# The adjacency product of the last graph layer in two float32r parts, with the matrix loaded again in pieces by POOL's queue

## Chip, cores and metric

The kernel runs on one core of a Trainium2 chip. The time is device microseconds of one execution of the whole program, as the median of three runs; lower is better.

## What is computed

A network of four layers on 16 graphs (B) of 1024 nodes (N) with 128 features (D). Each layer normalises the rows of x, applies relu, computes a graph operation with the adjacency matrix, and adds the result to x:

```python
# layer 0: three sage convolutions on a thinned adjacency (adj with some neighbours skipped)
# layer 1: attention, 4 heads of 32 features
scores = einsum('chqd,chkd->chqk', q, k) * SCALE + log(max(adj, EPS))
out    = softmax(scores) @ v @ Wo.T + bo
# layer 2: graph attention, 4 heads; e = leaky_relu(s_i + s_j), masked by adj, softmax over i
out    = einsum('bijh,bihd->bjhd', alpha, Wh)
# layer 3: normalised product of the adjacency
A_hat  = adj + eye(n);  d_inv = sum(A_hat, 2) ** -0.5
h      = einsum('bnm,bmf->bnf', d_inv[:, :, None] * A_hat * d_inv[:, None, :], h)
out    = h @ W.T + b
```

The adjacency holds zeros and ones. All inputs and the result are float32, and products keep about float32's precision: where a matrix operand is exact in a narrow type (the adjacency), the other operand is split into several narrow parts whose products are added up in PSUM.

## The kernel before, in words

The program has three stages: the thinning of the adjacency (up to some 680 us), the convolutions (to some 1550 us), and the attention stage, `attentions_plain`, in which layers 1 to 3 run for all 16 graphs. (A slower path behind a test at the end isn't taken with these inputs.) Only the attention stage is changed.

The attention stage is a set of seven jobs, written as Python generators, which go over the graphs b one after another and run interleaved:

- `matrices`: loads a graph's adjacency in eight row blocks (tile `a`, SP's queue), turns it into a one-byte tile `A` of 128 x 8 x 1024 (L1318, ACT), checks that it is zero or one (L1322, DVE) and symmetric (L1329 to L1335, PE and ACT; `junk2` takes the unused output). Four tiles `A` (pool `f_adj`).
- `before`: ends layer 0 and makes q, k, v of layer 1 (L1362 to L1391).
- `attend`: scores and exponentials of layer 1 (L1416 to L1429). It reads `A`.
- `values`: the weighted sums and the denominators (L1452), the reciprocal of the denominators into `rden` (L1458), and their product into `oT` (L1460).
- `positive` and `gat`: layer 2. `positive` makes masks `pm` on DVE (L1503), `gat` multiplies them with bf16 parts on PE (L1563 and L1578), and sums the results on DVE (L1566, L1581). POOL multiplies `vals` with exponentials `ex` (L1543). Both jobs read `A`.
- `gcn`: layer 3. `normal` normalises the rows of x, scaled by d_inv, into `g` (bn_stats on DVE, a power on POOL at L1275, eight activations on ACT at L1282). POOL adds the bias to x (L1610). Then `g` is split into three bf16 parts, half by half (L1615 to L1621: ACT, DVE, ACT, DVE). For each half `hf` of the columns, 8 row blocks times 3 parts are multiplied with `A` (L1632, 24 matmuls of 512 columns), and 4 blocks times 3 parts with the identity, which adds the eye of A_hat (L1636, 12 matmuls of 128 columns). ACT copies the sum to `aggT` (L1639), a product with W follows (L1303), and DVE and POOL finish the rows.

The order of instructions on each engine is fixed when the program is built. Each job yields, ahead of every step, the engine, a planned duration, the time at which its inputs are planned to be there, and whether it takes or gives back one of two PSUM banks (`bank`, pool `f_sum`). `in_order` always takes the step that can start first by that plan; among equals PE's steps come later and the job furthest behind its share goes first:

```python
start = max([free[engine], needs] + [min(pools[pool]) for pool, change in tiles(j) if change > 0])
key = (start, engine == "PE", j["did"] / j["per"] + j["lag"])
```

On the chip every engine then runs its own list strictly in that order, and waits on semaphores where an operand isn't there or a buffer isn't free. DMAs on SP's queue are issued by an engine that computes nothing; DMAs issued by POOL stand in line with POOL's arithmetic. A job also waits for others while the plan is made; `matrices` and `before` start graph b as follows:

```python
while done["gcn"] < b - 3 or done["attend"] < b - 1:
    yield
```

Of the kernel before, what the change touches and what calls it, by code (L numbers as in the profile page):

```python
# [5 lines left out]

F32 = mybir.dt.float32
F16 = mybir.dt.float16
BF16 = mybir.dt.bfloat16
F8 = mybir.dt.float8e4  # L10
# [8 lines left out]
P = 128  # L19
# [1194 lines left out]
def attentions_plain(tc, x, spill, final, ready_weights, adj, deg, trouble, eye, out, scores, bound, reach):  # L1214
    nc = tc.nc
    with ExitStack() as ctx:
# [3 lines left out]
        psa = ctx.enter_context(tc.tile_pool(name="f_acc", bufs=2, space=PSUM))  # L1220
        psg = ctx.enter_context(tc.tile_pool(name="f_sum", bufs=2, space=PSUM))
        xp = ctx.enter_context(tc.tile_pool(name="f_x", bufs=4))
        adp = ctx.enter_context(tc.tile_pool(name="f_adj", bufs=4))
        lp = ctx.enter_context(tc.tile_pool(name="f_load", bufs=2))
        ep = ctx.enter_context(tc.tile_pool(name="f_exp", bufs=2))
        pmp = ctx.enter_context(tc.tile_pool(name="f_pos", bufs=2))
        w2 = ctx.enter_context(tc.tile_pool(name="f_work2", bufs=2))
        w1 = ctx.enter_context(tc.tile_pool(name="f_work1", bufs=1))

        ident = cp.tile([P, P], F32, name="ident")  # L1230
        nc.sync.dma_start(ident, eye)
        ident16 = cp.tile([P, P], BF16, name="ident16")
        nc.vector.tensor_copy(ident16, ident)
        minus16 = cp.tile([P, P], BF16, name="minus16")
# [8 lines left out]
        def bank(pool=psg, name="sum"):  # L1243
            return pool.tile([P, HN], F32, name=name)
# [63 lines left out]
        def matrices():  # L1308

            for b in range(B):  # L1310
                while done["gcn"] < b - 3 or done["attend"] < b - 1:
                    yield
                m = adp.tile([P, NB, N], F8, name="A")
                for i in range(NB):
                    t = yield "ACT", 1.3, 0.0, 0
                    a = lp.tile([P, N], F32, name="a")
                    nc.sync.dma_start(a, adj[b, i * P:(i + 1) * P, :])
                    nc.scalar.activation(m[:, i, :], a, AF.Relu, accum_out=deg[:, b, i:i + 1], saturate=False)  # L1318
                    yield "DVE", 1.32, 0.0, 0
                    junk = lp.tile([P, N], F8, name="junk", bufs=1)  # L1320

                    nc.vector.scalar_tensor_tensor(junk, a, 0.0, a, op0=ALU.is_gt, op1=ALU.not_equal,  # L1322
                                                   accum_out=trouble[:, b, i, 0:1], saturate=False)
                    for hf in range(2):
                        w = min(HN, (i - 4 * hf) * P)
                        if w > 0:
                            e = yield "PE", 0.1 + w / 1024, t, 1
                            ps = bank()
                            nc.tensor.matmul(ps[:, :w], ident16, m[:, i, hf * HN:hf * HN + w], start=True, stop=False)  # L1329
                            for j in range(w // P):  # L1330
                                nc.tensor.matmul(ps[:, j * P:(j + 1) * P], m[:, 4 * hf + j, i * P:(i + 1) * P], minus16,
                                                 start=False, stop=j == w // P - 1)
                            yield "ACT", 0.8, e, -1
                            junk = lp.tile([P, HN], BF16, name="junk2", bufs=1)
                            nc.scalar.activation(junk[:, :w], ps[:, :w], AF.Abs, accum_out=trouble[:, b, i, 1 + hf:2 + hf])  # L1335

                t = yield "DVE", 0.2, 0.0, 0
                nc.vector.tensor_scalar(dinv[:, b], deg[:, b], 1.0, None, op0=ALU.add)
                yield "POOL", 1.7, t, 0
                nc.gpsimd.tensor_tensor(dinv[:, b], dinv[:, b], minus_half, op=ALU.pow)  # L1340
                A[b] = m
# [92 lines left out]
        def values():  # L1434

            free, n = 0.0, 0
            for b in range(B):
                oT = w1.tile([P, N], F32, name="oT")
                for hf in range(2):
                    cols = slice(hf * HN, (hf + 1) * HN)  # L1440
                    for k in range(NB):
                        while n not in exps:
                            yield
                        es, e = exps[n]
                        e = yield "PE", 1.85, max(e, free), 0
                        if k == 0:
                            acc, den = [bank(psa, "acc") for _ in range(2)]
                        va = ready[b][4]
                        for ps, one in ((acc, False), (den, True)):
                            for hd in range(H):  # L1450
                                r = slice(hd * HD, (hd + 1) * HD)
                                nc.tensor.matmul(ps[r], ones if one else va[:, k, r], es[:, hd],  # L1452
                                                 start=k == 0, stop=k == NB - 1)
                        taken[n] = e
                        n += 1
                    rden = w1.tile([P, HN], F32, name="rden")
                    e = yield "DVE", 3.4, e, 0
                    nc.vector.reciprocal(rden, den)  # L1458
                    free = yield "DVE", 0.7, e, 0
                    nc.vector.tensor_tensor(oT[:, cols], acc, rden, op=ALU.mult)  # L1460
                xt = ready[b][1]
                t = yield from natural_times(oT, free, wo, "DVE", lambda c, ps: nc.vector.tensor_tensor(
                    xt[:, c, :], xt[:, c, :], ps, op=ALU.add))
# [43 lines left out]
        def gat():  # L1507
            for b in range(B):
# [26 lines left out]
                shared[b, "sc"] = (hT, minus, m)  # L1535

                e = yield "ACT", 0.5, e, 0
                ex = small.tile([P, 2, NB, 8], F32, name="ex", bufs=2)
                nc.scalar.activation(ex[:, 0], sc, AF.Exp)
                nc.scalar.activation(ex[:, 1], sc, AF.Exp, scale=SLOPE)  # L1540
                for k in range(2):
# [60 lines left out]
        def gcn():  # L1602
            for b in range(B):
# [4 lines left out]
                t = yield from normal(xt, t, g, dinv[:, b])  # L1608
                yield "POOL", 2.4, 0.0, 0
                nc.gpsimd.tensor_tensor(xt, xt, per_col(b3r), op=ALU.add)  # L1610
                parts = w1.tile([P, 3, NB, D], BF16, name="gparts")
                for m in range(2):
                    half = slice(4 * m, 4 * m + 4)
                    e = yield "ACT", 0.6, t, 0
                    nc.scalar.copy(parts[:, 0, half], g[:, half])  # L1615
                    e = yield "DVE", 0.7, e, 0
                    nc.vector.tensor_tensor(g[:, half], g[:, half], parts[:, 0, half], op=ALU.subtract)
                    e = yield "ACT", 0.6, e, 0
                    nc.scalar.copy(parts[:, 1, half], g[:, half])
                    e = yield "DVE", 0.7, e, 0  # L1620
                    nc.vector.tensor_tensor(parts[:, 2, half], g[:, half], parts[:, 1, half], op=ALU.subtract)  # L1621
                t = e
                aggT = w1.tile([P, N], F32, name="aggT")
                for hf in range(2):
                    cols = slice(hf * HN, (hf + 1) * HN)
                    for m in range(NB):
                        if m % 2 == 0:
                            e = yield "PE", 1.3, t, 0 if m else 1
                            if m == 0:
                                ps = bank()  # L1630
                        for k in range(3):
                            nc.tensor.matmul(ps, parts[:, k, m, :], A[b][:, m, cols], start=m == 0 and k == 0, stop=False)  # L1632
                    e = yield "PE", 0.7, t, 0
                    for m in range(4):
                        for k in range(3):
                            nc.tensor.matmul(ps[:, m * P:(m + 1) * P], parts[:, k, 4 * hf + m, :], ident16,  # L1636
                                             start=False, stop=m == 3 and k == 2)
# [190 lines left out]
```

## Time and profile before

| | |
|---|---|
| three runs | 3955.3, 3951.44, 3953.14 us |
| median | 3953.14 us |
| profiled execution, first to last instruction | 3957.5 us |
| mean granted clock of PE | 0.941 |
| PE busy, 1500 us to the end (2457 us) | 2128.5 us |
| DVE, ACT, POOL busy there | 1662.0, 1593.6, 389.7 us |
| L1632, 768 matmuls of 512 columns | 176.3 us busy |
| L1636, 384 matmuls of 128 columns | 26.7 us busy |
| L1615 and L1619, ACT casts, 32 each | 19.7 and 19.9 us |
| L1617 and L1621, DVE subtractions, 32 each | 36.4 and 23.2 us |

The profile is of one execution, whose own time the page gives only as the span from the first to the last instruction. It lists busy time by engine, groups of instructions by line of the kernel with what ended the idle time before them, and the chain of work that ended last. Mean durations of matmuls contain a drain that overlaps the next one, so paces are read from start to start. For DMAs from POOL's queue there is also the time from issue to landing; for SP's and ACT's queues there is none.

### The profile page before, as it was taken

The page shows a single profiled execution, that of the slowest core. Times are in us where ns is not written, and L with a number is a line of the kernel's source. Part 1 is how long each engine was busy: PE and PEld are TensorE (multiplying, and loading weights), DVE is VectorE, ACT ScalarE, POOL GpSimd, SP SyncE. Part 2 cuts the span into 40 slices and gives each one's busy share as a digit, 9 for nine tenths or more (in the row PEclk, how much of TensorE's full clock was granted, in tenths as well). Part 3 has the DMA queues.
Part 4 walks back from the last instruction along what each step waited for, and adds up shares of the span by engine and source line. Part 5 has one row for each costly group of instructions (what it writes and reads, how often), then busy time and mean ns, then how long its engine had stood idle before and what let it go on. Part 6 is the DMA issues. An engine that isn't in the chain of part 4 may idle for free.

```text
span 3957.5 us, 65696 instructions
## 1 busy us (share of the span) xinstructions
PE 3428.3 (87%) x26692; PEld 1955.4 (49%) x26692; DVE 2524.1 (64%) x4782; ACT 2391.7 (60%) x3961; POOL 804.0 (20%) x680
## 2 busy tenths in 40 slices
PE   4888887899999987788989998998898899898875
PEld 2556565445555556334445544544454454554443
DVE  4988784553343444337767766876775776686676
ACT  3788764453333345786677677667667667667630
POOL 6545521210000011101112021112102112211111
PEclk9999986999999998899999999999999999999987
DMA  9632223443333313311222221212212222121000
GB/s 108 42 22 16 13 82 119 155 169 129 129 120 133 130 61 126 100 59 38 75 62 62 70 75 54 68 62 67 68 60 65 64 65 65 54 65 49 17 22 23
DMA packets 182498, 293.19 MB, mean 74 GB/s; under 512 B 77468, under 2 KB 124456, under 8 KB 173992
## 3 DMA queue, kind: packets, MB, share of 16 engines
q1 hardware_dynamic: 91944, 221.69, 17.4%
q0 software_dynamic: 79728, 24.66, 7.7%
q10 hardware_dynamic: 10512, 42.54, 2.7%
q8 instruction: 211, 3.46, 0.4%
q14 instruction: 103, 0.84, 0.1%
HBM read 287.98 MB, written 51.19 MB: 86 GB/s over the span
## 4 chain that ended last, share of the span: by engine, by line
PE 60%; DVE 18%; ACT 11%; DMA 5%; POOL 4%; issue 3%; SPq 0%; ACTq 0%; POOLq 0%; DVEq 0%
PE g L1040 12%; PE acc L1452 11%; PE sum L1578 8%; PE t L1421 5%; PE sum L1632 4%; PE sum L1563 4%; DVE pm L1503 3%; DMA rows<-in_adj_dram 3%; ACT e L1429 2%; PE sum L1365 2%; DVE rows L882 2%; DVE r L835 2%; PE o L1089 2%; PE o L1090 2%; DVE rden L1458 1%
## 5 line engine op out<-in xcount | busy, mean ns | idle before, releaser
L1429 ACT ACTIVATE e<-t 128x1024 f32<-128x1024 f32 x512 | 506.8, 1022 | 516.6 <-PE t L1421 467.3
L1503 DVE SCALAR_TENSOR_TENSOR pm<-dst,minus,A 128x1024 fp8e4<-128x1024 f32 x512 | 668.2, 1329 | 9.0 <-DMA dst<-scores 9.0
L1040 PE MATMUL g<-C,parts 128*128 128x512 fp8e4 x2304 | 524.8, 383 | 18.7 <-DVE aggT L1042 11.6
L1416 ACT ACTIVATE t<-A 128x2048 f32<-128x2048 fp8e4 x256 | 483.0, 1887 | 4.0 <-ACT dst L1483 0.6
L1578 PEld LDWEIGHTS <-pm 128*128 128x128 fp8e4 x4096 | 349.3, 98 | 178.0 <-issue 141.4
L1578 PE MATMUL sum<-parts,pm 128*128 128x198 bf16 x4096 | 399.5, 252 | 42.1 <-DVE pm L1503 29.3
L1452 PE MATMUL acc<-e,va 128*32 128x512 f32 x2048 | 356.7, 633 | 64.2 <-ACT e L1429 61.5
L1040 PEld LDWEIGHTS <-parts 128*128 128x128 bf16 x2304 | 224.1, 99 | 265.6 <-issue 9.7
L1452 PE MATMUL acc<-e,ones_hd 128*32 128x512 f32 x2048 | 343.5, 615 | 0.7 <-DVE oT L1460 0.7
L1421 PE MATMUL t<-qT,kT 32*128 32x512 f32 x2048 | 299.0, 654 | 21.2 <-ACT t L1416 20.8
L1581 DVE TENSOR_REDUCE pos<-sum 128x132 f32<-128x396 f32 x256 | 144.6, 566 | 177.7 <-PE sum L1578 177.5
L1042 DVE TENSOR_TENSOR aggT<-g,rdb 128x512 f32<-128x512 f32 x96 | 66.2, 690 | 271.6 <-PE g L1040 271.5
L1563 PE MATMUL sum<-parts,A 128*128 128x396 bf16 x1024 | 203.4, 342 | 19.7 <-DVE tot L1566 17.6
L1045 POOL TENSOR_TENSOR nrm<-nrm,minus_half 128x8 f32<-128x8 f32 x48 | 78.5, 1636 | 596.2 <-DVE nrm L1103 587.7
L835 DVE TENSOR_TENSOR r<-ya,both 128x512 bf16<-128x512 f16 x184 | 139.2, 771 | 89.9 <-ACT ya L832 89.2
L1632 PE MATMUL sum<-A,gparts 128*128 128x512 fp8e4 x768 | 176.3, 386 | 23.1 <-ACT gparts L1615 17.7
L1275 POOL TENSOR_TENSOR ln_st<-ln_st,minus_half 128x8 f32<-128x8 f32 x48 | 94.6, 1970 | 446.4 <-DVE ln_st L1273 406.2
L882 DVE SCALAR_TENSOR_TENSOR rows<-y,thirty,rows 128x1024 fp8e4<-128x1024 f16 x128 | 169.4, 1331 | 24.5 <-ACT y L874 23.9
L1100 ACT ACTIVATE sq<-o 128x512 f32<-128x512 f32 x96 | 55.1, 595 | 205.5 <-PE o L1093 126.3
L885 POOL TENSOR_TENSOR own<-rows,lower 128x256 bf16<-128x256 fp8e4 x128 | 110.1, 871 | 327.4 <-DVE rows L882 205.0
L872 PE MATMUL big<-tri,rows 128*128 128x256 fp8e4 (+3 forms) x896 | 171.6, 312 | 1.0 <-issue 0.4
L1322 DVE SCALAR_TENSOR_TENSOR junk<-a 128x1024 fp8e4<-128x1024 f32 x128 | 159.3, 1244 | 20.5 <-DMA a<-in_adj_dram 20.2
(291 smaller groups left out, 6691.5 us busy)
## 6 DMA issues: line engine op xcount, KB each, us to landing
a<-in_adj_dram SPq DMA_DIRECT2D x128, 512.0 KB
C<-kept SPq DMA_DIRECT2D x48, 1024.0 KB
dst<-scores SPq DMA_DIRECT2D x64, 512.0 KB
rdb<-rdeg SPq DMA_DIRECT2D x48, 512.0 KB
spill<-hT ACTq DMA_DIRECT2D x48, 512.0 KB
kept<-rows ACTq DMA_DIRECT2D x16, 1024.0 KB
h_a<-spill SPq DMA_DIRECT2D x64, 256.0 KB
hT_a<-spill SPq DMA_DIRECT2D x16, 512.0 KB
```

The costliest lines, as they stand in the source:

```text
L835: nc.vector.tensor_tensor(r, ya, both[:, 1, :, None].to_broadcast([P, G, P]), op=ALU.is_equal)
L872: nc.tensor.matmul(ps[:, k * P:], lhs, triF[:, :HN - k * P], start=k == 0, stop=k == 3)
L882: nc.vector.scalar_tensor_tensor(row, y16, hh[:, g:g + 1], row, op0=ALU.not_equal, op1=ALU.mult, saturate=False)
L1040: nc.tensor.matmul(ps, parts[:, k, j, :], C[:, j, cols], start=j == 0 and k == 0, stop=j == NB - 1 and k == 2)
L1416: nc.scalar.activation(s, A[b][:, k, None, cols].to_broadcast([P, H, HN]), AF.Copy, scale=16.0)
L1421: nc.tensor.matmul(s[:, hd], kT[r, k * P:(k + 1) * P], qT[r, cols], start=False, stop=True, skip_group_check=True)
L1429: nc.scalar.activation(es[:, hd:hd + 2], s[:, hd:hd + 2], AF.Exp, scale=SIGMA)
L1452: nc.tensor.matmul(ps[r], ones if one else va[:, k, r], es[:, hd], start=k == 0, stop=k == NB - 1)
L1503: nc.vector.scalar_tensor_tensor(pm[:, i, :], dst[hd], minus[:, i, hd:hd + 1], A[b][:, i, :], op0=ALU.is_ge, op1=ALU.mult, saturate=False)
L1563: nc.tensor.matmul(ps[:, :3 * H * W], A[b][:, i, j * P:(j + 1) * P], parts4[:, i, :, :, W:], start=i == 0, stop=i == NB - 1)
L1578: nc.tensor.matmul(ps[:, jj * 6 * W:(jj + 1) * 6 * W], pm[:, i, (j + jj) * P:(j + jj + 1) * P], flat(parts4[:, i, hd]), start=i == 0, stop ...
L1632: nc.tensor.matmul(ps, parts[:, k, m, :], A[b][:, m, cols], start=m == 0 and k == 0, stop=False)
```

## The change

In `gcn`, `g` is split into two float32r parts instead of three bf16 parts, so for each half one ACT copy and one DVE subtraction remain. The product no longer reads the one-byte tile `A`. The adjacency is loaded again from DRAM for it, as eight float32r pieces per graph (`wide`, two row blocks by 512 columns, 512 KB), by DMAs from POOL's queue, into three buffers. Two pieces are asked for while the parts are made, and each further one in the plan after the matmuls of the piece two places ahead of it. For each half of the columns there are 16 matmuls of 512 columns and 8 of 128 columns with a float32r identity.

To make room, `A` has three tiles instead of four, and `matrices` waits for `gat` of the graph three back, which is now the last job that reads the tile. The reciprocal goes straight into `oT`, `junk2` is one byte wide, `ex` has one buffer, and the identity is loaded by way of a tile `a`. The planned durations in `gcn` are changed to go with it.

```diff
-        adp = ctx.enter_context(tc.tile_pool(name="f_adj", bufs=4))
+        adp = ctx.enter_context(tc.tile_pool(name="f_adj", bufs=3))
+        wp = ctx.enter_context(tc.tile_pool(name="f_wide", bufs=3))
...
-        ident = cp.tile([P, P], F32, name="ident")
-        nc.sync.dma_start(ident, eye)
+        loaded = lp.tile([P, N], F32, name="a")[:, :P]
+        nc.sync.dma_start(loaded, eye)
+        identr = cp.tile([P, P], F32R, name="identr")
+        nc.vector.tensor_copy(identr, loaded)
+        ident = identr.bitcast(F32)
...
-                while done["gcn"] < b - 3 or done["attend"] < b - 1:
+                while done["gcn"] < b - 3 or done["gat"] < b - 2 or done["attend"] < b - 1:
...
-                            junk = lp.tile([P, HN], BF16, name="junk2", bufs=1)
-                            nc.scalar.activation(junk[:, :w], ps[:, :w], AF.Abs, accum_out=trouble[:, b, i, 1 + hf:2 + hf])
+                            junk = lp.tile([P, HN], F8, name="junk2", bufs=1)
+                            nc.scalar.activation(junk[:, :w], ps[:, :w], AF.Abs, accum_out=trouble[:, b, i, 1 + hf:2 + hf], saturate=False)
...
-                    nc.vector.reciprocal(rden, den)
+                    nc.vector.reciprocal(oT[:, cols], den)
                     free = yield "DVE", 0.7, e, 0
-                    nc.vector.tensor_tensor(oT[:, cols], acc, rden, op=ALU.mult)
+                    nc.vector.tensor_tensor(oT[:, cols], acc, oT[:, cols], op=ALU.mult)
...
-                ex = small.tile([P, 2, NB, 8], F32, name="ex", bufs=2)
+                ex = small.tile([P, 2, NB, 8], F32, name="ex", bufs=1)
...
-                parts = w1.tile([P, 3, NB, D], BF16, name="gparts")
+                wide = {}
+
+                def fetch(hf, m):
+                    if hf < 2:
+                        wide[hf, m] = wp.tile([P, 2, HN], F32R, name="wide")
+                        nc.gpsimd.dma_start(wide[hf, m], adj[b, m * P:(m + 2) * P, hf * HN:(hf + 1) * HN]
+                                            .rearrange("(t p) m -> p t m", p=P))
+
+                parts = w1.tile([P, 2, NB, D], F32R, name="gparts")
                 for m in range(2):
                     half = slice(4 * m, 4 * m + 4)
                     e = yield "ACT", 0.6, t, 0
                     nc.scalar.copy(parts[:, 0, half], g[:, half])
                     e = yield "DVE", 0.7, e, 0
-                    nc.vector.tensor_tensor(g[:, half], g[:, half], parts[:, 0, half], op=ALU.subtract)
-                    e = yield "ACT", 0.6, e, 0
-                    nc.scalar.copy(parts[:, 1, half], g[:, half])
-                    e = yield "DVE", 0.7, e, 0
-                    nc.vector.tensor_tensor(parts[:, 2, half], g[:, half], parts[:, 1, half], op=ALU.subtract)
+                    nc.vector.tensor_tensor(parts[:, 1, half], g[:, half], parts[:, 0, half], op=ALU.subtract)
+                    w = yield "POOL", 0.8, 0.0, 0
+                    fetch(0, 2 * m)
                 t = e
+                w += 2.5
                 aggT = w1.tile([P, N], F32, name="aggT")
                 for hf in range(2):
                     cols = slice(hf * HN, (hf + 1) * HN)
-                    for m in range(NB):
-                        if m % 2 == 0:
-                            e = yield "PE", 1.3, t, 0 if m else 1
-                            if m == 0:
-                                ps = bank()
-                        for k in range(3):
-                            nc.tensor.matmul(ps, parts[:, k, m, :], A[b][:, m, cols], start=m == 0 and k == 0, stop=False)
-                    e = yield "PE", 0.7, t, 0
+                    for m in range(0, NB, 2):
+                        e = yield "PE", 0.87, max(t, w), 0 if m else 1
+                        if m == 0:
+                            ps = bank()
+                        for mm in range(m, m + 2):
+                            for k in range(2):
+                                nc.tensor.matmul(ps, parts[:, k, mm, :], wide[hf, m][:, mm - m], start=mm == 0 and k == 0, stop=False)
+                        ahead = 8 * hf + m + 4
+                        if ahead < 2 * NB:
+                            w = 2.5 + (yield "POOL", 0.8, 0.0, 0)
+                            fetch(ahead // NB, ahead % NB)
+                    e = yield "PE", 0.9, t, 0
                     for m in range(4):
-                        for k in range(3):
-                            nc.tensor.matmul(ps[:, m * P:(m + 1) * P], parts[:, k, 4 * hf + m, :], ident16,
-                                             start=False, stop=m == 3 and k == 2)
+                        for k in range(2):
+                            nc.tensor.matmul(ps[:, m * P:(m + 1) * P], parts[:, k, 4 * hf + m, :], identr,
+                                             start=False, stop=m == 3 and k == 1)
```

More of the change, by code (lines that the diff above doesn't have):

```diff
@@ L7 @@
 F32 = mybir.dt.float32
+F32R = mybir.dt.float32r
 F16 = mybir.dt.float16
@@ L1455, in values @@
                         n += 1
-                    rden = w1.tile([P, HN], F32, name="rden")
                     e = yield "DVE", 3.4, e, 0
-                    nc.vector.reciprocal(rden, den)
+                    nc.vector.reciprocal(oT[:, cols], den)
                     free = yield "DVE", 0.7, e, 0
-                    nc.vector.tensor_tensor(oT[:, cols], acc, rden, op=ALU.mult)
+                    nc.vector.tensor_tensor(oT[:, cols], acc, oT[:, cols], op=ALU.mult)
                 xt = ready[b][1]
```

## The prediction

> **What bounds the kernel now.** I read the shares of busy time first, then the chain that ended last, then stretches of the attention stage (1500 us to the end), and last the order of TensorE (PE) there.
>
> ```profile
> PE 3428.3 (87%) x26692; PEld 1955.4 (49%) x26692; DVE 2524.1 (64%) x4782; ACT 2391.7 (60%) x3961; POOL 804.0 (20%) x680
> ...
> PE 60%; DVE 18%; ACT 11%; DMA 5%; POOL 4%; issue 3%; SPq 0%; ACTq 0%; POOLq 0%; DVEq 0%
> ...
> L1632 PE MATMUL sum<-A,gparts 128*128 128x512 fp8e4 x768 | 176.3, 386 | 23.1 <-ACT gparts L1615 17.7
> ```
> ```profile
> 2000.00:2500.00 500.00, 458.07 (x3408) 235.55 (x3404) 361.63 (x551) 359.53 (x502) 88.14 (x45) 0.97 0.22 69
> 2500.00:3000.00 500.00, 456.36 (x3487) 244.02 (x3479) 365.74 (x538) 345.60 (x462) 84.86 (x42) 0.97 0.20 62
> ```
> In the second view the columns are stretch, length, busy PE, weight loads, DVE, ACT, POOL, then clock, DMA share, GB/s. PE is busy 91% in mid-stage, DVE and ACT some 72%, POOL 17%, DMA 21%: PE bounds. The changed product (L1632) is 4% of the chain, some 158 of its 176 us, so a microsecond there counts about 0.9. How fast it runs is in PE's timeline (start, length, engine, line):
> ```profile
> 2726.09 5.34 PE L1632 MATMUL sum<-A,gparts 128*128 128x512 fp8e4 x24
> 2731.27 0.83 PE L1636 MATMUL sum<-ident,gparts 128*128 128x128 bf16 x12
> 2732.04 1.02 PE L1481 MATMUL sum<-hT,weights 128*4 128x512 f32 x2
> ```
> From start to start: 5.18/24 = 0.216 us for 512 columns, 0.77/12 = 0.064 for 128. (The 386 ns of the row counts the drain, which overlaps.)
>
> **What the Trainium skill says.** "DMA: Bandwidth & Descriptors", "SWDGE vs HWDGE vs iDMA": a float32r destination always casts, and only GpSimd's queue casts; so the pieces must go through POOL. Same page, "Anatomy of one DMA": about 2.0 us plus bytes at 436 GB/s, 3.2 us for 512 KB; the trace has 4.9 for that size from POOL's queue, and I use the trace. "TensorE: Matmul & The Clock Gate", "Back-to-back issue gap": N/2.4 + 2.5 ns, 216 ns for 512; the trace agrees (0.216). No page gives float32r's matmul rate.
>
> **Change, part by part.**
> PE, removed: 768 x 0.216 + 384 x 0.064 = 165.9 + 24.6 = 190.5 us.
> PE, added: 512 float32r matmuls of 512 columns, 256 of 128. The trace has none. It has float32, where each matmul leaves two records:
> ```profile
> 2660.67 1.05 PE L1383 MATMUL sum<-hT_a,weights 128*128 128x512 f32 x2
> ...
> 2670.59 1.08 PE L1303 MATMUL sum<-weights,hT_a 128*128 128x128 f32 x8
> ```
> The next groups start at 2661.64 and 2671.51: about 0.44 us a record at 512 columns, 0.115 at 128. Bounds for 512 columns: 0.216 (the present product; nothing in the array is faster) and 0.44 (a float32 half); a full float32 matmul is 0.88. I take 0.216, one pass, half the records of float32 and at the pace of the present operands; this is an assumption, and the fourth case below prices its failure. For 128 columns: 0.064 to 0.23; I take one float32 record, 0.115, because a 4-byte weight load (0.19 us recorded in L1303, against 0.10 for bf16) has to fit in. Sum 110.6 + 29.4 = 140.0. Gain 50.5 us.
>
> The wait added: each of 8 pieces a batch (512 KB, two row blocks by 512 columns) lands before its four matmuls, 0.86 us of work, and PE's queue is in order, so everything behind waits too: scores, values, sums. Three buffers: piece p is fetched once piece p-3 has been used. The prices for landing:
> ```profile
> xt<-in_x_dram POOLq DMA_DIRECT2D x15, 512.0 KB, 4.9
> ...
> rows<-in_adj_dram POOLq DMA_DIRECT2D x16, 128.0 KB, 9.8
> ...
> rows<-in_adj_dram POOLq DMA_DIRECT2D x32, 32.0 KB, 3.1
> ```
> The last two cast to one byte, so they read 512 and 128 KB. The 9.8 is with eight in flight: pairs of 512 + 448 KB were issued every 2.5 us, some 390 GB/s, so casting itself isn't slow. Low end: 32 KB late in that stage took 2.7 us; 384 KB more at that rate is 1.0; 0.3 for the last matmul's drain and the hop to POOL: 4.0. High end 6, about the first big one (6.5, at start-up). I take 5.0: 4.9, less 0.3 for a shorter issue (0.6 against 0.93 us on POOL), plus 0.4 for drain, hop and the other DMAs.
>
> Cover comes from the order of PE's instructions in the changed kernel, each group priced by its start-to-start time in this trace (scores 0.27 a matmul, values 0.23, pos 0.09, tot 0.18). Pieces 3 to 7 of 16 batches are 80. Between the end of p-3 and the start of p stand: under 2 us of PE work for 12 of them, 2 to 3 for 12, 3 to 5 for 15, more for 41. Often p0 to p3 or p4 to p7 follow one another with nothing between, cover 8 x 0.216 = 1.7. Walking the order and pushing everything back by each shortfall, stalls sum to 30 us at a landing of 3.5, 42 at 4.0, 53 at 4.5, 66 at 5.0, 79 at 5.5, 93 at 6.0. I take 66.
>
> Pieces 0 to 2 find free buffers, but stand in POOL's queue behind the addition of L1610:
> ```profile
> 2715.56 2.35 POOL L1610 TENSOR_TENSOR x<-x,weights 128x1024 f32<-128x1024 f32 x1 [4.17 <-ACT h_g L1282]
> ```
> It ends at 2717.9 and the product began at 2726.1: 8.2 us of cover against 5, so nearly hidden. In the last batch nothing covers: L1610 ends at 3930.4, the product began at 3928.5. I take 5 us for all (0 to 10).
>
> POOL: 128 issues x 0.6 = 77 us on an engine busy 17%. A fetch that waits for PE holds up what is behind it: the norms' powers (L1275) and gat's vals (L1543, 1.9 us, twice, between p5 and p7 in seven batches). The gat waits for vals; PE has attention work meanwhile, so 0, and 0.5 us a batch (8 us) at the high end; if that cover goes, the following tot sums start late.
>
> ACT and DVE lose 32 casts of 0.62 (L1619) and 32 subtractions of 0.72 (L1621), 43 us of engines busy 72%; 6 us on the path (0 to 11, a quarter), mostly where parts are late for PE. Nothing is next but the pieces.
>
> Edits with no cost: reciprocals straight into oT, one-byte junk2, ex with one buffer (a batch's sums end long before the next exponentials) and the float32r identity change no instruction's work. Three adjacency buffers instead of four: they now wait for gat, not gcn. In both orders the last check of a matrix stands only a few us of PE work ahead of its first scores (least: 4 before, 2 after), covered by the values of the batch before; gone, it is a few us a batch. 64 MB more DMA in 2450 us adds some 26 GB/s to 65.
>
> Sum: -50.5 + 66 + 5 - 6 = +14.5, times 0.9 = +13. The span is 3957.5, 4.4 above the median of 3953.1 (first to last instruction; what lies around isn't on the page). I add to the median: **3966 us**.
>
> **Rivals.**
> 1. Likeliest, 0.45: the landing wait takes the place of the removed matmuls, 3966 (3950 to 3985).
> 2. Other side, faster, 0.25: landing 3.5 to 4.0 us. Stalls 30 to 42, first pieces 2: -50.5 + 36 + 2 - 6 = -18.5, some 3936. It decides from the point where stalls are 51, a landing of 4.4 us. For it: longer runs (2 KB against xt's 512 bytes), and PE's own gaps (9%) lengthen the cover. Against: the same queue took 4.9, and 21% of DMA is busy.
> 3. Longer landings and a blocked POOL, 0.18: 93 + 10 + 8 - 50.5 = +60, 4007 at 6 us; about 3995. For it: adjacency rows of 512 KB go at the same time on SP's queue. Against: DMA has room.
> 4. Float32r isn't one pass, 0.12: 512 x 0.44 + 29.4 = 254.7, +64; longer matmuls cover more, so stalls fall to 28: +91 times 0.9, 4035. The change then doesn't do what it says. For it: four bytes a row to stream; against: half the parts of float32.
>
> **How the numbers follow.** About 0.2% (8 us) is what measurement tells from no change: 3945 to 3961. Faster: nearly all of 2, 0.25. Same: a third of 1, 0.16. Slower: 0.59. Range 3932 to 4015: leaves out the fast tail of 2 and most of 4.
>
> **What would show it.** Groups of 16 float32r matmuls at 0.216 each, or 0.44. PE idle before the wide product put down to the DMA of the pieces: some 66 us in all, most at p3 and p7; landing of the pieces near 4.7. POOL's issue 0.6. PE busy down by about 50 with the span up. Wrong if the landing is under 4.4, if DVE and ACT relief reaches the path, or if other groups (scores, tot) come to wait for a late matrix.

## The result, and the profile after

| | before | after |
|---|---|---|
| median (4 runs each) | 3952.29 us | 4088.51 us |
| lowest, highest | 3943.21, 3955.3 us | 4076.98, 4095.65 us |
| profiled execution, first to last instruction | 3957.5 us | 4080.5 us |
| mean granted clock of PE | 0.941 | 0.927 |

The ratio is 1.0342, with a 95% interval of 1.0316 to 1.0368 (intervals stand in brackets from here on): 136 us slower, where 13 us were forecast. The direction was right, the size was not.

The same lines of the page as before, shares, chain, product and landing of a piece:

```profile
PE 3463.2 (85%) x26308; PEld 2015.2 (49%) x26308; DVE 2494.6 (61%) x4751; ACT 2378.5 (58%) x3929; POOL 889.8 (22%) x808
...
PE 51%; DVE 12%; DMA 6%; ACT 5%; issue 4%; POOL 2%; POOLq 0%; ACTq 0%; SPq 0%; DVEq 0%
...
L1643 PE MATMUL sum<-wide,gparts 128*128 128x512 f32 x512 | 156.0, 444 | 81.4 <-DMA wide<-in_adj_dram 76.0
...
wide<-in_adj_dram POOLq DMA_DIRECT2D x128, 512.0 KB, 4.8
```

PE has 384 matmuls fewer and is busy 35 us more; its share of the chain fell from 60% to 51%. The product waits 76 us for pieces, which land in 4.8 us (the median). The two stretches in mid-stage, with the columns as before:

```profile
2000.00:2500.00 500.00, 429.31 (x3004) 232.75 (x3001) 331.00 (x509) 325.92 (x456) 109.28 (x77) 0.92 0.30 93
2500.00:3000.00 500.00, 426.91 (x2971) 227.74 (x2970) 328.61 (x469) 311.35 (x423) 92.83 (x62) 0.93 0.28 88
```

PE does 13% fewer matmuls in the same 500 us, is busy some 30 us less, and its clock is down from 0.97 to 0.92. POOL and DMA have more to do, but are far from full. What such a stretch looks like is in PE's timeline of the third graph (start, length, engine, line; in brackets the idle time before, and what ended it):

```profile
2175.10 1.02 PE L1527 MATMUL sum<-weights,hT 128*128 128x136 f32 x4 [0.34 <-ACT h L1533]
2178.37 4.67 PE L1643 MATMUL sum<-wide,gparts 128*128 128x512 f32 x12 [2.25 <-DMA wide<-in_adj_dram]
2185.95 2.08 PE L1643 MATMUL sum<-wide,gparts 128*128 128x512 f32 x4 [2.90 <-DMA wide<-in_adj_dram]
2187.83 1.80 PE L1651 MATMUL sum<-identr,gparts 128*128 128x128 f32 x8
...
2193.12 1.21 PE L1643 MATMUL sum<-wide,gparts 128*128 128x512 f32 x4
```

Pieces 0 to 2 stand together and run in 4.67 us, then piece 3 is 2.90 us late, and its four matmuls take 2.08 us where piece 4, with other work ahead of it, takes 1.21. The first stall, 2.25 us, is before piece 0. The records of the clock say why the groups get slow: half clock from 2172.3 to 2175.7, from 2179.1 to 2182.6 and from 2186.0 to 2192.8, full clock between. So the 2.08 us lie wholly at half clock.

To compare kernels I take the attention stage from 1480 us to the last matmul in the trace: PE's busy time, how much of that lies in half-clock stretches (half of it is taken as what the lower clock costs), and PE's idle time.

| profiled run | last matmul ends | PE busy | of it at half clock | idle |
|---|---|---|---|---|
| before | 3947.0 | 2145.1 | 188.1 | 321.9 |
| after | 4069.3 | 2176.9 | 306.5 | 412.4 |

So +122 us is +90 idle, +59 by the clock (half of 118), and 27 less for the work itself. That is a description and not yet a cause: idle time can come from the wait for pieces, or from the place in which everything else now stands.

### The profile page after: what moved, and what is told of

The parts are those of the page before. It is cut to its first block, busy times and chain, and to the rows that moved or that the text cites. A ratio compares the mean times of both kernels' runs of the same rounds, so it can differ in the third digit from the quotient of the medians.

```text
span 4080.5 us, 65190 instructions
## 1 busy us (share of the span) xinstructions
PE 3463.2 (85%) x26308; PEld 2015.2 (49%) x26308; DVE 2494.6 (61%) x4751; ACT 2378.5 (58%) x3929; POOL 889.8 (22%) x808
## 3 DMA queue, kind: packets, MB, share of 16 engines
q8 instruction: 208, 3.41, 0.3%
## 4 chain that ended last, share of the span: by engine, by line
PE 51%; DVE 12%; DMA 6%; ACT 5%; issue 4%; POOL 2%; POOLq 0%; ACTq 0%; SPq 0%; DVEq 0%
PE g L1041 11%; PE acc L1457 10%; PE sum L1582 8%; PE t L1426 5%; DMA wide<-in_adj_dram 4%; PE sum L1567 4%; DVE pm L1507 3%; PE sum L1370 2%; PE o L1090 2%; ACT e L1434 2%; PE o L1091 1%; PE sum L1308 1%; PE sum L1643 1%; DVE oT L1462 1%; DVE bs L1270 1%
## 5 line engine op out<-in xcount | busy, mean ns | idle before, releaser
L1507 DVE SCALAR_TENSOR_TENSOR pm<-dst,minus,A 128x1024 fp8e4<-128x1024 f32 x512 | 656.4, 1305 | 8.0 <-DMA dst<-scores 8.0
L1426 PE MATMUL t<-qT,kT 32*128 32x512 f32 x2048 | 311.0, 679 | 39.3 <-ACT t L1421 39.0
L1643 PE MATMUL sum<-wide,gparts 128*128 128x512 f32 x512 | 156.0, 444 | 81.4 <-DMA wide<-in_adj_dram 76.0
L1567 PEld LDWEIGHTS <-A 128*128 128x128 fp8e4 x1024 | 93.4, 98 | 180.9 <-issue 106.0
L1327 DVE SCALAR_TENSOR_TENSOR junk<-a 128x1024 fp8e4<-128x1024 f32 x128 | 170.6, 1333 | 19.6 <-DMA a<-in_adj_dram 19.3
L1462 DVE RECIPROCAL oT<-acc 128x512 f32<-128x512 f32 x32 | 107.3, 3353 | 112.1 <-PE acc L1457 112.1
```

The costliest lines, as they stand in the source:

```text
L1426: nc.tensor.matmul(s[:, hd], kT[r, k * P:(k + 1) * P], qT[r, cols], start=False, stop=True, skip_group_check=True)
L1462: nc.vector.reciprocal(oT[:, cols], den)
L1507: nc.vector.scalar_tensor_tensor(pm[:, i, :], dst[hd], minus[:, i, hd:hd + 1], A[b][:, i, :], op0=ALU.is_ge, op1=ALU.mult, saturate=False)
L1567: nc.tensor.matmul(ps[:, :3 * H * W], A[b][:, i, j * P:(j + 1) * P], parts4[:, i, :, :, W:], start=i == 0, stop=i == NB - 1)
L1643: nc.tensor.matmul(ps, parts[:, k, mm, :], wide[hf, m][:, mm - m], start=mm == 0 and k == 0, stop=False)
```

## The experiments

First theories. Theory 1: PE's stalls for pieces, and the lower clock after them, make the loss. Rival 1: the new order of the work, or three matrices in advance instead of four. Rival 2: the float32r matmuls themselves. Rival 3: the transfers and a held POOL. All times are medians of four runs (e16: twenty). Each ratio is to runs of the kernel before that were taken beside the experiment's, since the kernel before itself has medians from 3945 to 3952 us.

**e1, no reload.** The waits for pieces, their traffic and POOL's issues are away; the planned order is kept.
```diff
+        fixed = [wp.tile([P, 2, HN], F32R, name="wide") for _ in range(3)]   # loaded once
...
-                        wide[hf, m] = wp.tile([P, 2, HN], F32R, name="wide")
-                        nc.gpsimd.dma_start(wide[hf, m], adj[b, ...])
+                        wide[hf, m] = fixed[m // 2 % 3]
```


> The three tiles are loaded once, before the loop over the batches, and never again; the planned order of everything else is that of the changed kernel. Left out: the matrix of each graph (the product uses rows of the first graph), so this is a time only. Theory 1 (the stalls before the pieces, and the lower granted clock after each of them, make the loss): no idle time of PE before the product's matmuls, the time at half clock in the attention stage back from 306 us to about 190, total 3920 to 3940 us. Rival 1 (the new order of the work or the three matrices in advance instead of four make it): 4030 us or more. Rival 2 (the float32r matmuls are slow or pull the clock down by themselves): the groups stay at 0.25 us a matmul, the time at half clock stays near 300 us, total 4000 us or more.

3988.61 us, ratio 1.0096 [1.0079, 1.0113]. The reload costs 97 us (1.0342 - 1.0096, times 3949). But without it the kernel is still 38 us slower than before, though its PE has less to do; its busy time at half clock is 246 us, against 188 before. Theory 1 explains two thirds at most, and something like rival 1 has to explain the rest.

**e2, three matrices in the kernel before.**
```diff
-        adp = ctx.enter_context(tc.tile_pool(name="f_adj", bufs=4))
+        adp = ctx.enter_context(tc.tile_pool(name="f_adj", bufs=3))
...
-                while done["gcn"] < b - 3 or done["attend"] < b - 1:
+                while done["gcn"] < b - 2 or done["gat"] < b - 2 or done["attend"] < b - 1:
```


> The kernel before with three tiles for the loaded adjacency instead of four, and the planner's gate moved from three batches to two, as the change does; the product stays in bfloat16. Theory 1: nothing to be seen, 3945 to 3965 us. Rival 1 (matrices that come late): 4000 us or more, with idle time of PE or DVE put down to the load of the adjacency.

4001.73 us, 1.0137 [1.012, 1.0154]: rival 1's side. No wait of PE is put down to a load of the adjacency, DVE's waits for one are 19.9 us against 20.2 before, and ACT's 30.1 against 19.9, so matrices that come late are not enough. (This gate is stricter than the change's, since here the last layer still reads `A`.)

**e4, loads that nobody reads.**
```diff
-                        wide[hf, m] = wp.tile([P, 2, HN], F32R, name="wide")
-                        nc.gpsimd.dma_start(wide[hf, m], adj[b, ...])
+                        wide[hf, m] = fixed
+                        spare = wp.tile([P, 2, HN], F32R, name="wide")     # two of them
+                        nc.gpsimd.dma_start(spare, adj[b, ...])
```


> The changed kernel with all its loads of pieces, from the same queue at the same places, but into two spare tiles that nothing reads; PE reads one tile that is loaded once. Left out: the matrix of each graph (the product uses rows of the first graph). It keeps the traffic and POOL's issues and takes away PE's waits. Theory 1: as with no reload at all, within 15 us of it, 3920 to 3950 us. Rival 3 (traffic and a held POOL): 4000 us or more.

4019.28 us, 1.0178 [1.0161, 1.0195]. It lies 32 us above no reload, not within 15: traffic and POOL do cost, as rival 3 said. The remaining 65 us up to the changed kernel are PE's waits for pieces and what follows from them. Between these two profiled runs, PE's idle time grows by 27 us and its half-clock busy time by 54, which costs 27: the stalls cost as much by the clock as by themselves. The other waits show where the 32 may come from. A row of such a view is what waited, what released it, and then us in total, times, and the longest. PE's waits for ACT's `t` (scores), without and with the loads:

```profile
PE t L1426 <- ACT t L1421: 40.2, 26, 4.0
```
```profile
PE t L1427 <- ACT t L1422: 60.7, 28, 6.8
```
The gat's `vals` are made by POOL, and POOL's queue is held at the loads. In e1 ACT never waits for `vals`; in e4 it does:

```profile
ACT parts L1554 <- POOL vals L1550: 34.3, 9, 6.9
```
The waits of PE, ACT and DVE for other transfers didn't grow: 86 us in e1, 72 in e4. That points to the held POOL and not to the traffic, but no run separates the two; another queue than POOL's wasn't tried for these loads, so no run shows either that they must go by it. POOL is held 151.6 us in e4, where a load waits for an earlier load of its tile, and in the changed kernel, where it waits for PE,

```profile
POOL wide L1620 <- PE sum L1643: 170.4, 54, 10.9
```
54 times, up to 10.9 us. In the changed kernel ACT has no wait for `vals`, and PE's for `t` are 39.0 us, as without loads. So the stalls for pieces there take the place of these waits, and the 32 and the 65 us needn't be two costs that add up in every order.

**e3, an honest plan.**
```diff
+                for p in range(3):
+                    lands[p] = 4.2 + (yield "POOL", 0.75, 0.0, 0)
+                    fetch(0, 2 * p)
...
-                        e = yield "PE", 0.87, max(t, w), 0 if m else 1
+                        e = yield "PE", 0.97, max(t, lands[p]), 0 if m else 1
...
+                        if p + 3 < 8:
+                            lands[p + 3] = 4.2 + (yield "POOL", 0.75, e, 0)
+                            fetch((p + 3) // 4, 2 * ((p + 3) % 4))
```


> The changed kernel with the landing told to the planner as it was measured: the three first pieces are asked for after the parts, each later piece is planned on POOL when the matmuls on its tile end, it counts as landed 4.2 us after its issue of 0.75 us, and each group of four matmuls waits in the plan for its own piece, so that other work of PE is laid between the groups. Theory 1: the idle time before the product falls from 81 us to under 30, the time at half clock falls with it, total 3935 to 3985 us. Rival 1 (order and three matrices): still about 4060 us or more. Rival 3 (the transfers themselves, by contention with other loads or by holding POOL, make the loss): idle time before the product falls but the total stays above 4040 us.

3970.1 us, 1.0051 [1.0034, 1.0067]: the same work and the same loads as the changed kernel, 115 us faster. The waits for pieces fell from 76.0 to 46.8 us, of which 24.0 are one wait in the last graph, where nothing is left to lay between:

```profile
PE sum L1645 <- DMA wide<-in_adj_dram: 46.8, 13, 24.0
```
But waits that fell by 29 don't explain 115. Busy time at half clock fell by 73 and idle by 71 us, much of it elsewhere than at the pieces. The plan also put everything else in a new order, so the 115 us aren't the price of the waits alone.

Next theories, for the part that isn't the reload. Theory 2: the added gate on `gat`. Theory 3: the weight of the last layer in the planner (17.0), which divides its planned PE work in the planner's key; that work fell from 13.4 to 10.4 us a graph, so the layer seems late and is taken first.

**e5, the gate alone, in the kernel before.**
```diff
-                while done["gcn"] < b - 3 or done["attend"] < b - 1:
+                while done["gcn"] < b - 3 or done["gat"] < b - 2 or done["attend"] < b - 1:
```
The same line changes in `before`, the job.

> The kernel before, with four tiles for the loaded adjacency and the bfloat16 product as they were, and only the added condition of the change on when the matrices of a batch may be planned (attention over the edges at most two batches behind). Theory 2 (the loss that is left without the reload comes from that gate): 3980 to 4000 us, with no wait for a load of the adjacency. Theory 3 (it comes from the weight of the last layer in the planner): as before, 3940 to 3960 us.

4016.45 us, 1.0188 [1.0168, 1.0208]: 74 us slower, with no work added, no buffer taken away and no transfer. That is more than theory 2 said, and against theory 3.

**e6, float32r alone.**
```diff
-        adp = ctx.enter_context(tc.tile_pool(name="f_adj", bufs=3))
-        wp = ctx.enter_context(tc.tile_pool(name="f_wide", bufs=3))
+        adp = ctx.enter_context(tc.tile_pool(name="f_adj", bufs=4))
...
-                while done["gcn"] < b - 3 or done["gat"] < b - 2 or done["attend"] < b - 1:
+                while done["gcn"] < b - 3 or done["attend"] < b - 1:
...
-    nc.tensor.matmul(ps, parts[:, k, mm, :], wide[hf, m][:, mm - m], ...)
+    nc.tensor.matmul(ps, parts[:, k, mm, :], parts[:, 0, 4 * hf:4 * hf + 4].rearrange("p c d -> p (c d)"), ...)
```


> The changed kernel with four tiles and the old gate, and with no piece loaded: the float32r product takes the parts themselves as its moving operand, so that it needs no buffer. Left out: the adjacency of the product. What stays is two float32r parts instead of three bfloat16 parts, in the planner's new costs. Theory 2 (gate): 3905 to 3930 us, the saved matmuls show. Theory 3 (weight of the last layer in the planner, unchanged at 17.0 though its planned work fell from 13.4 to 10.4): 3960 us or more, in spite of 30 us less work on PE.

3979.15 us, 1.0089 [1.0071, 1.0107]: without gate and without loads still slower than before. Theory 2 doesn't hold: the gate costs 74 us with the old planned costs and, from here to e1 (which has three tiles as well), 3 us with the new ones. It has no price of its own.

**e7 and e8, another weight,** in the changed kernel and in the honest plan.
```diff
-                      (1, 54.0, gat()), (2.5, 17.0, gcn())], {"sum": 2})
+                      (1, 54.0, gat()), (2.5, 13.1, gcn())], {"sum": 2})     # e8: 14.2
```


> The changed kernel with the weight of the last layer in the planner lowered from 17.0 to 13.1, in proportion to its planned PE work (17.0 x 10.36 / 13.4). Theory 2: no gain, 4070 to 4095 us. Theory 3: 4020 to 4050 us, the 40 us that the kernel without reload still lost come back.

> The honest plan of the landings with the weight lowered to 14.2 (17.0 x 11.16 / 13.4). Theory 2: 3960 to 3980 us, no gain. Theory 3: 3920 to 3945 us, faster than the kernel before.

4094.96 us, 1.0391 [1.0366, 1.0415], and 4015.06 us, 1.0168 [1.0141, 1.0195]. Theory 3 falls: e7 gains nothing, and e8 is 45 us slower than the honest plan with 17.0, where it should have been 25 to 50 us faster. Theory 2 had e7 right and not e8. All these kernels have nearly the same work on PE. That led to theory 4: the order of instructions decides by tens of us, and that of the kernel before is a good one.

**e9, float32r in the old order.** As e6, but `gcn` yields the steps and costs of the kernel before (also for the casts that are gone), so that PE, ACT and POOL keep the old order of everything else.
```diff
-                        e = yield "PE", 0.87, max(t, w), 0 if m else 1
+                        e = yield "PE", 1.3, t, 0 if m else 1
...
+                    e = yield "ACT", 0.6, e, 0
+                    e = yield "DVE", 0.7, e, 0
```


> As the float32r product on its own parts (no piece loaded, four tiles, old gate), but with the planner's steps and costs of the kernel before, so that every other instruction stands in the order of the kernel before on each engine. Left out: the adjacency of the product. Theory 4 (the order that the planner finds for the new costs is worse than the old one, by 40 to 70 us, and the float32r product by itself is a gain): 3905 to 3930 us. Rival (the float32r matmuls cost more elsewhere than they save): 3945 us or more.

3921.12 us, 0.9933 [0.9913, 0.9954]: 26 us faster than before, and 62 us faster than e6, whose instructions are the same in another order. The product's row in e9:

```profile
L1633 PE MATMUL sum<-gparts 128*128 128x512 f32 x512 | 131.4, 408 | 22.5 <-ACT gparts L1618 17.7 <-ACT aggT L1641 3.1 <-DVE gparts L1620 1.7
```
What the two orders do to the stage, length and PE's busy time first, clock and DMA last, e9 and then e6:

```profile
2000.00:2500.00 500.00, 456.20 (x3413) 250.99 (x3413) 359.27 (x521) 360.84 (x503) 89.56 (x45) 0.97 0.22 71
```
```profile
2000.00:2500.00 500.00, 432.69 (x3146) 236.43 (x3147) 354.52 (x536) 342.64 (x480) 92.77 (x47) 0.95 0.21 66
```
e9 has 267 matmuls more in the same 500 us. From 1480 us on PE is idle 325 us in e9 and 372 in e6, and 193 and 221 us of its busy time lie at half clock. No single wait carries it. The same rows of PE's waits in e9 and then in e6:

```profile
PE acc L1456 <- ACT e L1433: 61.5, 42, 7.6
...
PE t L1425 <- ACT t L1420: 24.2, 21, 2.9
...
PE sum L1566 <- DVE tot L1569: 17.3, 18, 2.7
...
PE sum L1333 <- ACT A L1322: 11.9, 8, 3.6
PE sum L1307 <- DVE oT L1463: 8.8, 6, 2.2
...
PE sum L1566 <- DVE parts L1558: 2.4, 2, 2.0
```
```profile
PE acc L1456 <- ACT e L1433: 57.2, 48, 6.5
PE t L1425 <- ACT t L1420: 34.9, 29, 4.0
...
PE sum L1566 <- DVE tot L1569: 24.8, 18, 4.0
PE sum L1333 <- ACT A L1322: 23.7, 11, 6.0
PE sum L1566 <- DVE parts L1558: 23.7, 4, 13.5
PE sum L1307 <- DVE oT L1463: 21.3, 5, 9.1
```
Several hand-overs from ACT and DVE to PE are covered worse in e6, by 8 to 21 us each; the longest, for `e`, is covered a little better.

**e10 and e11, the kernel before with one number of the plan changed.** No instruction is added or removed.
```diff
-                      (1, 54.0, gat()), (2.5, 17.0, gcn())], {"sum": 2})
+                      (1, 54.0, gat()), (2.5, 16.0, gcn())], {"sum": 2})     # e10
...
-                            e = yield "PE", 1.3, t, 0 if m else 1
+                            e = yield "PE", 1.2, t, 0 if m else 1            # e11
```


> The kernel before with one number of the planner changed: the weight of the last layer 16.0 instead of 17.0. The work is the same. Theory 4 (the order before is a chosen one, and a near order costs some 20 to 70 us): 3970 us or more. Rival (orders differ by chance by less than 10 us): 3940 to 3960 us.

> The kernel before with one number of the planner changed: a pair of row blocks of the product planned at 1.2 us of PE instead of 1.3. The work is the same. Theory 4: 3970 us or more. Rival: 3940 to 3960 us.

3966.95 us, 1.0053 [1.0032, 1.0074], 3 us short of the bound of theory 4 and outside the rival's, and 4005.62 us, 1.015 [1.0129, 1.0171]. With the gate of e5 these are three near orders of the old work: 21, 59 and 74 us slower. Theory 4 holds. e11's last matmul ends 45 us later than before, with 26 us more idle time, 27 by the clock (half of 53.6), and 8 less for the rest.

**e12 to e16, more orders of the honest plan:** the weight of the last layer 18.0, 15.0 or 20.0, its lag 2.0 instead of 2.5, or 5.5 us instead of 4.2 to the landing.

> The honest plan of the landings with the weight of the last layer 18.0 instead of 17.0. The work is that of the honest plan. Theory 4 (the order decides by some tens of us, without a trend in the weight): anywhere from 3930 to 4020 us, more than 8 us away from 3970. A trend (a heavier weight is better, since 14.2 gave 4015 and 17.0 gave 3970): 3925 to 3955 us.

> The honest plan with the weight of the last layer 15.0. Order theory: 3930 to 4020 us, not the 3970 of 17.0 and not the 4015 of 14.2 by rule. Fixed cost of the loads: 3965 to 3980 us. A trend with the weight (the lighter, the slower): 3985 to 4010 us.

> The honest plan with the weight of the last layer 20.0. Order theory: 3930 to 4020 us. Fixed cost of the loads: 3965 to 3980 us. Trend with the weight: below 3965 us.

> The honest plan with the lag of the last layer in the planner 2.0 batches instead of 2.5, so that it is planned earlier. Order theory: 3930 to 4020 us. Fixed cost of the loads: 3965 to 3980 us.

> The honest plan with 5.5 us from issue to landing instead of 4.2, above the median of the landings (4.87). If the waits that are left for late pieces (26 us outside the last batch) are what is missing: 3940 to 3955 us, with under 10 us of them. Order theory: 3930 to 4020 us, and the time does not follow those waits.

| | us | ratio | PE's waits for pieces |
|---|---|---|---|
| e3, 17.0 | 3970.1 | 1.0051 [1.0034, 1.0067] | 46.8 us |
| e12, 18.0 | 3972.69 | 1.007 [1.0047, 1.0093] | 47.6 us |
| e13, 15.0 | 4009.22 | 1.0155 [1.0129, 1.0181] | 45.6 us |
| e14, 20.0 | 3991.24 | 1.0105 [1.0082, 1.0129] | 54.8 us |
| e15, lag 2.0 | 3995.58 | 1.0117 [1.0088, 1.0146] | 45.3 us |
| e16, landing 5.5 | 3961.36 | 1.0029 [1.0018, 1.0039] | 55.4 us |

e12's expectation rested on a new order, and there was none: 18.0 gives the order of 17.0 on every engine. So it repeats e3, and shows that the same order gives the same time, on another chip. The others scatter from 3961 to 4009 us, and the fixed cost of 3965 to 3980 holds for none of the four new orders. e13 lies in the range of a trend with the weight, e14 (20.0, slower than 17.0) doesn't; a valley around 17.0, with 4015, 4009, 3970 and 3991 us at 14.2, 15.0, 17.0 and 20.0, isn't ruled out by four weights. e16 was meant to cut the waits for pieces; its order has more of them than e3's and is the fastest.

**e17 and e18, fetches across graphs,** with 5.5 and 4.2 us to the landing.
```diff
-                        if p + 3 < 8:
-                            lands[p + 3] = 5.5 + (yield "POOL", 0.75, e, 0)
-                            fetch((p + 3) // 4, 2 * ((p + 3) % 4))
+                        if 8 * b + p + 3 < 8 * B:
+                            q = (p + 3) % 8
+                            lands[q] = 5.5 + (yield "POOL", 0.75, e, 0)
+                            fetch(b + (p + 3) // 8, q)
```


> The honest plan with 5.5 us to the landing, and the fetches run on across batches: the tile that a piece of one batch leaves takes the piece three further on, of the next batch at the end. Fixed cost of the loads: 3935 to 3955 us, as PE's waits for pieces fall from 57 to under 35 us (24.0 to 17.7 in the last batch). Order theory: a new order, 3930 to 4010 us, whatever these waits do.

> The same with 4.2 us to the landing. Fixed cost of the loads: within 10 us of the one with 5.5. Order theory: 3930 to 4010 us, more than 10 us away from it.

3989.74 us, 1.011 [1.0058, 1.0162], and 3995.05 us, 1.011 [1.0079, 1.0142]. The waits for pieces fall to 18.7 us in e17; in the last graph the fetch no longer comes last, but the casts (17.7 us), as before:

```profile
PE sum L1644 <- DMA wide<-in_adj_dram: 18.7, 13, 4.7
...
PE sum L1644 <- ACT gparts L1626: 17.7, 1, 17.7
```
And yet it is 28 us slower than e16, which waits three times as long (55.4 us): against the fixed cost, and as the order theory has it. The two landings differ by 5 us; here the fixed cost, which said within 10, was right, and the order theory, which said more than 10, was not. No version with the loads beats the kernel before.

## Why the prediction was wrong, step by step

The kernels e9, e6, e1, e4 and after form a ladder (differences of ratios times 3949 us; each step is good to about 10 us). before and e9 have one planned order, e1, e4 and after another, and e6 a third:

| step | measured | forecast |
|---|---|---|
| before to e9: float32r product, fewer casts | -26 | 0.9 x (-50.5 - 6) = -51 |
| e9 to e6: the order that the new costs give | +62 | 0 |
| e6 to e1: gate, three tiles | +3 | 0 |
| e1 to e4: traffic, loads in POOL's queue | +32 | 0 |
| e4 to after: PE waits for pieces | +65 | 0.9 x (66 + 5) = +64 |
| sum | +136 | +13 |

**The step that failed** is the one that took the rest of the order as given: "Edits with no cost", and the sum after it. The prediction walked the new order of PE's instructions to find the cover of each piece, but asked nothing else of it. That the change also altered planned costs, and with them the place of everything in the stage, was priced at nothing, and this is the largest unforeseen term: 62 us with e9 against e6, the same instructions. It has the size of the 21, 59 and 74 us by which the old work gets slower when one number or gate of its plan is changed. Since every near order of the old work that was run is slower than the kernel before, some loss was to be expected; its size is chance, as far as the runs show.

**POOL's issues** were priced at "so 0", 8 us at the high end. An issue took 0.72 us, 0.6 were taken. From e1 to e4 they cost 32, together with the traffic. The doubt was named (gat's `vals` behind a fetch that waits), and in e4 the waits for `vals` and for the scores grew. So the cover named for it, attention work of PE, seems not to have been enough; that it was this and not the traffic isn't shown. Rival 3 of the prediction had this mechanism, at a quarter of its size.

**The stalls** were right in kind, and in sum by luck. Landing: 5.0 taken, 4.8 in the trace. Pieces 3 to 7 wait 43 us, against 66, nearly all of it at p3 and p7 as foretold, 1.7 us at a time. Pieces 0 to 2 wait 33 us, against 5; 24.0 of them are one wait in the last graph, where the kernel before waits 17.7 us for the casts, so some 16 are new. That is 59 us instead of 71, and not all of it is new idle time on PE, since other waits shrink. In return the stalls cost more through the clock, which the prediction left out: 27 us of idle time and 27 of half clock make most of the 65. The clock is also why PE's busy time rose by 35 us, where the prediction had it fall by about 50.

**The float32r product** gained half of what was forecast. Removed, from start to start at full clock in the trace before: 768 x 0.217 + 384 x 0.062 = 190.5 us, as worked out. Added, in e9: 0.238 us for 512 columns, not 0.216, and 0.116 for 128, as taken: 121.9 + 29.7 = 151.6 instead of 140.0, so 39 us are saved instead of 50.5. By the prediction's own reckoning that and the 6 us for ACT and DVE make 0.9 x 45 = 41; measured are 26, by the interval 18 to 34. Where the other 15 stay isn't shown; the relief of ACT and DVE can't be seen.

**Rivals.** The fourth (two passes, 0.44 us) doesn't hold, with 0.238 measured. The second (a landing under 4.4) had its condition unmet. That a change of the plan alone costs as much as the waits for the transfers, 62 against 65 us, was in none of them.

**What stays open.** Why one order is 60 us better than its neighbours: e9 against e6 shows many small waits and more half-clock time, not one place. Whether the held POOL or the traffic makes the 32 us. And whether some order of the version with the loads would beat the kernel before: eight distinct orders that the honest plan gave lie at 3961 to 4015 us, three near orders of the old work at 3967 to 4016. By these few, the two kinds of work are about equal when neither has a picked order; what e9 gains, the loads take.

## What to carry to other kernels

Where a planner fixes the order, a change of planned costs or of a gate is a change to every engine: keep the old steps and costs in one build, so that the new instructions stand in the old order, and only then judge the instructions. Measure how much the kernel moves when a planned number that matters little is changed, and believe no gain or loss under that. A transfer that has to land ahead of an in-order engine needs its real latency in the plan: eight orders planned with it (in two of them the fetches also run across graphs) took 3961 to 4015 us, two planned without it (the changed kernel and e7) 4089 and 4095. That is some 100 us on average, more than the 74 us that the order alone did here, while a single one of these orders doesn't tell the price of the latency.

## What the hardware showed

A float32r matmul of 512 columns takes 0.238 us from start to start (e9, mostly in groups of 16) where the fp8-against-bf16 one took 0.217, and its weight load is recorded with 193 ns against 99. In groups of four, as in the changed kernel, it is 0.27.

Short stalls are followed by half clock. "TensorE: Matmul & The Clock Gate", "HAM oscillation — how this bites in real kernels", in the Trainium skill, gives as the rule no idle gaps of PE over about 3.4 us; here gaps of 2.25 and 2.90 us were each followed by half clock, in stretches of 3.4 us and multiples of it. The stretch of 3.4 us ahead of the first, 2175.7 to 2179.1, held 2.25 us of idle time.

The whole attention stage says the same. The clock of its records changes only at the edges of a fixed raster of 3.41 us. I sort the stretches of this raster from 1480 us on by the idle time between PE's matmuls in them, and count how often the next stretch is at half clock:

| this stretch | its idle time | before | after |
|---|---|---|---|
| full clock | 2.0 us or more | 27 of 27 | 47 of 47 |
| full clock | 1.25 to 2.0 us | 13 of 39 | 18 of 46 |
| full clock | less | 0 of 571 | 3 of 544 |
| half clock | 0.5 us or more | 43 of 43 | 46 of 48 |
| half clock | less | 1 of 41 | 5 of 71 |

So in these traces the sum of idle time within a stretch decides, and not the length of one gap: in the changed kernel 7 of the 47 had no gap of 2 us, and 19 stretches that touched such a gap, but held less than 1.25 us of it, were all followed by full clock. And the way back is narrow: after a half-clock stretch with 0.5 us or more of idle time, half clock stayed in 89 of 91 cases.
